# A four-layer graph network on one core: the first group's x loaded by rows and turned by TensorE, and layer 3's sums scaled on ScalarE instead of VectorE

## The chip, the core and the metric

The kernel runs on one core of a Trainium2 chip. The core has five engines that work side by side, each through its own queue in order: TensorE (PE, matrix products and transposes, written to PSUM), VectorE (DVE), ScalarE (ACT), GpSimd (POOL) and SyncE (SP, which here only issues DMAs). The profile gives the loading of TensorE's stationary operand a row of its own, PEld. The metric is the device time of one execution in microseconds (us). Before the change it is 2847.82 us, the median of 3 runs (2847.09 to 2848.99).

## What is computed

There are 128 graphs of 128 nodes with 256 features, and an adjacency matrix for each. Four layers follow one another; each ends in a residual sum and a layer norm.

```python
x = layernorm(x + gat(x, adj, L0_W, a_src, a_dst))       # attention of 4 heads, elu
x = layernorm(x + gated(x, adj, weight, w_ih, ...))      # 3 rounds: sum over neighbours, GRU cell
x = layernorm(x + relational(x, adj, weight, bias))      # adj == 1 .. 4, here only the value 1 occurs
# layer 3: attention of one head
Wh = einsum('bni,oi->bno', h, W)
e = leaky_relu((Wh @ a1)[:, :, None] + (Wh @ a2)[:, None, :], 0.2)
attention = softmax(where(adj > 0, e, -9e15), axis=-1)
x = layernorm(h + elu(einsum('bij,bjo->bio', attention, Wh)))
```

## The kernel before

The graphs are worked in 33 groups: one of 2 graphs, 31 of 4, one of 2. A group passes through stages that are Python generators: `loads` (its DMAs), `head` (layer 0), four interleaved lanes for layer 1 (`chunk_0`, `chunk_1` with the gates' elementwise work, `reset_and_new`, `new_and_update` with the gates' products, line 590), and `tail` (layers 2 and 3). Several groups are under way at once. Which stage of which group takes its next step is written out by hand as strings of letters: `START` for the beginning, `STEPS` for each of the periods in the middle, `END` for the end. `advance` takes one step, that is, runs a generator to its next `yield`. At the end every engine's instructions are tied to the order in which they were written (line 860), so no scheduler moves them: each engine does exactly what the strings say, in that order.

PSUM has eight banks. Two pairs hold the gates' sums (tags `sums` and `gate`); the other four (`OTHERS = 4`, line 26) form one ring under the tag `ps`, from which `bank()` hands out the next in turn, whoever asks. A tile of the ring may be written only when the reader of the tile four requests earlier is done. `psb` tiles (line 419) come out of the same ring.

Layer 0 needs x with features on the partitions. The method is the same for all groups: `load_x_squares` (line 151) issues eight DMAs that put 32x32 squares into `x0s`, so that a VectorE transpose within squares (line 437) gives xT; `head` multiplies xT by `w0` (line 450, TensorE), copies the result to `wh` (line 453, ScalarE), and goes on to scores, softmax and the weighted sum. `load_rows` (line 149) brings x by rows as well, for the residual. For the first group these loads are issued before all else on SP, while ScalarE's queue issues the loads of the weights (lines 182 to 222) before its first real work, which is `above` (line 443).

After the first products of the first group comes `fold` (line 269), which folds weights of layer 1 into one another; its first matmuls (line 276) multiply the loaded `w_hh` into the `sums` banks.

In layer 3, `tail` computes `em` (the unscaled exponentials) and `den` (their sums, then their reciprocals, line 801), turns `em` to `aT`, and multiplies it by `wh` for two graphs at a time into one `ps` bank (line 823). Line 826 scales this bank by the reciprocals into `o`, one VectorE operation of 128x512. `residual_elu_norm` then reads `o` (line 377, ScalarE).

Around line 826 other groups are at work. In the middle periods the two halves of a group are scaled at two places, some 6 us apart:

- The first stands on VectorE between line 353 (a norm's statistics) and line 618 (a gate's sum). On ScalarE that place lies between the `z` activation (line 642) and four exponentials of layer 0 (line 398), which are followed by `n` (line 654), `z` again and the norm's application to x2 (line 361, read by the products `rel` x `x2` of line 740).
- The second stands on VectorE between the scores of line 475 and line 394. On ScalarE that place lies between the copy of `h1N` (line 676, read by the neighbours' products of line 569, ps<-edge,h1N) and the two copies of `hr` (line 742, read by line 754).

Of the kernel before, what the change touches and what calls it, by code (L numbers as in the profile page):

```python
# [9 lines left out]
F32 = mybir.dt.float32  # L10
BF16 = mybir.dt.bfloat16
I32 = mybir.dt.int32
AF = mybir.ActivationFunctionType
ALU = mybir.AluOpType
AX = mybir.AxisListType

P = 128
N = 128
D = 256
C = D // P  # L20
# [60 lines left out]
def kernel(ctx: ExitStack, tc: tile.TileContext, a: dict, out: bass.AP):  # L81
    nc = tc.nc
# [8 lines left out]
    sp = ctx.enter_context(tc.tile_pool(name="work", bufs=1))  # L91
# [5 lines left out]
    def ring(pool, shape, dtype, tag, name, bufs):  # L97

        k = taken[tag] = (taken.get(tag, -1) + 1) % bufs
        return pool.tile(shape, dtype, tag=f"{tag}_{k}", name=name, bufs=1)  # L100

    def bank(*shape, tag="ps"):

        t = ring(pp, [P, 512], F32, tag, tag, OTHERS if tag == "ps" else GATES)
        n = 1
        for s in shape:
            n *= s
        if len(shape) == 1:
            return t[:, :n]
        names = "abcd"[: len(shape)]  # L110
        sizes = {k: s for k, s in zip(names[1:], shape[1:])}
        return t[:, :n].rearrange(f"p ({' '.join(names)}) -> p {' '.join(names)}", **sizes)

    def matmul(ps, lhsT, rhs, start=True, stop=True):
        nc.tensor.matmul(ps, lhsT, rhs, start=start, stop=stop)  # L115

    def transpose(ps, src):
        nc.tensor.transpose(ps, src, ident)  # L118
# [11 lines left out]
    def squares(t, src):  # L130


        for b in range(P // Q):
            nc.sync.dma_start(
                t[ts(b, Q)].rearrange("r (i s) -> r i s", s=Q),
                src.rearrange("(i r) m -> r i m", r=Q)[:, :, ts(b, Q)],
            )

    def load_adj(st):
        st["adj"] = ring(sp, [P, st["n"], N], I32, "adj", f"adj_{st['g']}", 3)  # L140
        nc.sync.dma_start(st["adj"], adj[st["graphs"]].rearrange("g n m -> n g m"))
# [5 lines left out]
    def load_rows(st):  # L147
        st["x0"] = sp.tile([P, st["n"], D], F32, tag="x0", name=f"x0_{st['g']}")
        nc.sync.dma_start(st["x0"], x[st["graphs"]].rearrange("g n d -> n g d"))

    def load_x_squares(st):
        st["x0s"] = sp.tile([P, C, st["n"] * N], F32, tag="x0s", name=f"x0s_{st['g']}")
        for c in range(C):
            squares(st["x0s"][:, c, :], x[st["graphs"]].rearrange("g n d -> (g n) d")[:, ts(c, P)])
# [12 lines left out]
    def layers():  # L167
        return {"layers": [{"h": {}, "a": {}, "gates": {}} for _ in range(L)], "h": {}}

    def state(g):  # L170
        by_pe = {"head": g == 0, "tail": g == NG - 1}
        return {"g": g, "graphs": spans[g], "n": sizes[g], "relations": 1, "by_pe": by_pe, **layers()}

    states = {0: state(0)}


    load_x_squares(states[0])
    load_adj(states[0])
    load_rows(states[0])

    w0 = cp.tile([P, C, D + 2 * H], F32, tag="w0", name="w0")
    nc.scalar.dma_start(w0[:, :, :D], a["L0_gnn_W"].rearrange("(c p) o -> p c o", p=P))
# [128 lines left out]
    def from_dram(t, d):  # L311

        squares(t, d)
        return t
# [117 lines left out]
    def head(st):  # L432

        g0, n, by_pe = st["g"], st["n"], st["by_pe"]["head"]
        xT = st["x0s"]
        flat = xT.rearrange("p c m -> p (c m)")
        nc.vector.transpose(flat, flat)  # L437
        yield
        nbias = absent(st["adj"], f"0_{g0}")
        yield  # L440
# [5 lines left out]
        for g in range(G):  # L446
            if g < n:
                ps = bank(D + 2 * H)
# [9 lines left out]
        den = ring(sp, [P, n * H], F32, "den0", f"den0_{g0}", 2)  # L458
        ems = {}
        for k in range(0, G, 2):  # L460
# [6 lines left out]
            for g in range(k, k + 2):  # L467
                ps = rows_of[g] = bank(H, N)
# [26 lines left out]
        y = ring(sp, [P, n, D], F32, "x1", f"x1_{g0}", 2)  # L495
        nc.vector.reciprocal(den, den)
        yield
        for k in range(0, G, 2):
# [5 lines left out]
            if by_pe:  # L504
                for j in range(2):
                    ps = bank(H, N)
# [3 lines left out]
            else:  # L510
                flat = aT.rearrange("p g h n -> p (g h n)")
# [3 lines left out]
            ps = bank(2, H, F)  # L515
# [170 lines left out]
    def tail(st):  # L686

        g0, n, x1, hT, relations = st["g"], st["n"], st["x1"], st["h"], st["relations"]
        by_pe = st["by_pe"]["tail"]
        if by_pe:  # L690
            yield
            yield
            y = sp.tile([P, n, D], F32, tag="x2", name=f"x2_{g0}")
            for c in range(C):
                ps = bank(n, N)
# [5 lines left out]
        else:  # L701
# [7 lines left out]
            y = sp.tile([P, n, D], F32, tag="x2", name=f"x2_{g0}")  # L709
            flat = from_dram(y.rearrange("p g d -> p (g d)"), d)  # L710
# [13 lines left out]
        flat = adj_T  # L724
        nc.vector.transpose(flat, flat)
        adj_T = adj_T.rearrange("p (g n) -> p g n", g=n)
        y = ring(sp, [P, n, D], F32, "x3", f"x3_{g0}", 2)
# [3 lines left out]
        for k in range(0, n, step):  # L731
# [5 lines left out]
            for c in range(C):  # L737
                ps = bank(step, relations, N)
# [8 lines left out]
            for pair in range(k, k + step, 2):  # L747
                graphs = range(pair, min(pair + 2, k + step))
                ps = bank(len(graphs), D)
# [26 lines left out]
        xT = st["x3T"]  # L776
        wh = sp.tile([P, n, D + 2], F32, tag="wh3", name=f"wh3_{g0}")
        for g in range(G):
            if g < n:
                ps = bank(D + 2)  # L780
# [9 lines left out]
        den = ring(sp, [P, n], F32, "den3", f"den3_{g0}", 2)  # L790
        ps = bank(n, N)
# [11 lines left out]
        if by_pe:  # L803
            yield
            yield
            ps = bank(n, N)
# [4 lines left out]
        else:  # L811
            d = to_dram(f"em3_{g0}", em)
            yield
            flat = from_dram(aT.rearrange("p g n -> p (g n)"), d)
# [3 lines left out]
        y = sp.tile([P, n, D], F32, tag="o", name=f"o_{g0}")  # L818
        for k in range(0, G, 2):
            if k < n:  # L820
                ps = bank(2, D)
                for g in range(k, k + 2):
                    matmul(ps[:, g - k, :], aT[:, g, :], wh[:, g, :D])
            yield
            if k < n:
                nc.vector.tensor_tensor(
                    y[:, k : k + 2, :], ps, den[:, k : k + 2].unsqueeze(2).to_broadcast([P, 2, D]), ALU.mult
                )
            yield
        yield from residual_elu_norm(y, "x3", st, "o", "3")  # L830
        nc.sync.dma_start(out[st["graphs"]].rearrange("g n d -> n g d"), st["o"])
# [1 line left out]


    STAGES = {"c": constants, "f": fold, "l": loads, "h": head, "t": tail}
    STAGES |= {"p": reset_and_new, "q": new_and_update, "u": chunk_0, "v": chunk_1}
    running = {}
# [36 lines left out]
    ps = bank(1)  # L874
# [4 lines left out]
    with tc.If(redo > 0):  # L879
        with tc.For_i(0, B, G) as first:  # L880

            graphs = bass.ds(first, G)

            st = {"g": "all", "graphs": graphs, "n": G, "relations": R, **layers()}
            st["by_pe"] = {"head": False, "tail": False}
            for stage in (loads, head):
                for _ in stage(st):
                    pass
            lanes = {which: STAGES[which](st) for which in "pquv"}
            for which, steps in [("u", 4), ("v", 6)] + IN_TURN * L:  # L890
                for _ in range(steps):
                    next(lanes[which], None)
            for _ in tail(st):
                pass
# [38 lines left out]
```

## Time and profile before

| | |
|---|---|
| median of 3 runs | 2847.82 us |
| the profiled execution | 2849.61 us |
| its span, first to last instruction | 2847.7 us |
| TensorE busy | 2744.5 us, 96% of the span |
| VectorE busy | 2290.5 us, 80% |
| ScalarE busy | 1734.5 us, 61% |
| GpSimd busy | 941.2 us, 33% |
| line 826 on VectorE | 64 times, 43.7 us, 683 ns each |
| line 437 for the first group | once, 0.71 us |

The profile follows one execution. The span is the time from its first to its last instruction. "Busy" adds up the time in which an engine worked; matmuls are pipelined, so that a matmul of 256 columns shows 0.38 us but the next one starts 0.22 us later. In a line of the timeline stand the start in us, the length, the engine, the line of the code, the operation, what it writes and reads (with buffer numbers left out), the shape and how many were merged; in brackets, how long the engine had been idle and which instruction released it. In a list of waits stand the waiting engine and line, the releasing one, the total of the waits in us, their number and the longest.

### The profile page before, as it was taken

Reading aid. Unit: us, or ns where it says so; the run is one execution under the profiler, and the core shown is the slowest. Engines: PE = TensorE matmul, PEld = TensorE weight load, DVE = VectorE, ACT = ScalarE, POOL = GpSimd, SP = SyncE. Lnnn points to the kernel's source line nnn. Section 1 sums busy time; section 2 is a strip of 40 time slices with the busy share of each in tenths; the row PEclk is TensorE's granted clock in tenths of the full one; section 3 lists DMA queues with packets and bytes.
Section 4 is the critical chain, followed back from the end, with each engine's and each line's share of the span. In section 5 each row is a group of like instructions: output and inputs, shape, how many; then the busy total and the mean of one; then the engine's idle time right before and its main releaser. Section 6 shows DMA issues by size and latency. Waiting matters only on the chain.

```text
span 2847.7 us, 44849 instructions
## 1 busy us (share of the span) xinstructions
PE 2744.5 (96%) x14486; PEld 2292.4 (81%) x14486; DVE 2290.5 (80%) x5334; ACT 1734.5 (61%) x4440; POOL 941.2 (33%) x925
## 2 busy tenths in 40 slices
PE   6899999999999999999999999999999999999986
PEld 4778888888888888888888888888888888888774
DVE  6678888878888878888878888888888887888765
ACT  3556666656666656666656666656666656666644
POOL 0223333323333323333323333423333333333331
PEclk9999999999999999999999999999999999999998
DMA  3344555444555344545344445444445444445321
GB/s 91 79 83 82 98 107 107 86 93 89 100 102 111 82 93 90 103 97 114 85 88 95 99 97 115 89 82 98 95 97 115 93 83 95 95 96 110 71 56 46
DMA packets 1179217, 264.01 MB, mean 93 GB/s; under 512 B 932065, under 2 KB 1178721, under 8 KB 1178977
## 3 DMA queue, kind: packets, MB, share of 16 engines
q1 hardware_dynamic: 1174448, 257.26, 45.1%
q10 hardware_dynamic: 4528, 3.81, 0.5%
q8 instruction: 118, 1.93, 0.3%
q14 instruction: 123, 1.00, 0.1%
HBM read 153.36 MB, written 107.61 MB: 92 GB/s over the span
## 4 chain that ended last, share of the span: by engine, by line
PE 75%; DVE 19%; issue 2%; POOL 1%; ACT 1%; DMA 1%; SPq 0%; DVEq 0%; POOLq 0%; ACTq 0%
PE gate L590 35%; PE ps L115 21%; PE sums L590 16%; DVE d L662 2%; PE ps L118 2%; DVE h3T L663 2%; DVE gate L618 2%; DVE h2T L663 2%; DVE n L652 1%; DVE aT L512 1%; DVE em L475 1%; DVE h0T L334 1%; DVE em L796 1%; POOL T_h L553 1%; DVE sums L610 1%
## 5 line engine op out<-in xcount | busy, mean ns | idle before, releaser
L590 PE MATMUL gate<-T_a,factors 128*128 128x256 f32 (+1 forms) x2376 | 683.1, 376 | 17.8 <-DVE T_a L553 16.9
L590 PE MATMUL gate<-T_h,factors_h 128*128 128x256 f32 (+1 forms) x2376 | 682.0, 377 | 12.3 <-DVE gate L618 8.9
L590 PEld LDWEIGHTS gate<-T_a,factors 128*128 128x128 f32 x2376 | 438.6, 190 | 91.1 <-DVE T_a L553 29.5
L590 PEld LDWEIGHTS gate<-T_h,factors_h 128*128 128x128 f32 x2376 | 428.8, 190 | 96.1 <-DVE gate L618 37.4
L590 PE MATMUL sums<-agT,factors 128*128 128x256 f32 (+1 forms) x1188 | 344.5, 376 | 2.3 <-ACT sums L600 1.4
L654 ACT ACTIVATE n<-n,bih 128x512 f32<-128x512 f32 (+1 forms) x198 | 139.5, 705 | 248.6 <-DVE n L652 248.6
L600 ACT COPY sums<-gate 128x256 f32<-128x256 f32 (+1 forms) x396 | 139.8, 353 | 204.7 <-PE gate L590 199.3
L361 ACT ACTIVATE x<-x,mr_x,rs_x 128x256 f32<-128x256 f32 x384 | 199.2, 589 | 90.9 <-DVE mr_x L356 90.9
L398 ACT ACTIVATE em<-em,nm 128x128 f32<-128x128 f32 x640 | 248.1, 392 | 8.3 <-DVE nm L395 5.4
L590 PEld LDWEIGHTS sums<-agT,factors 128*128 128x128 f32 x1188 | 219.5, 190 | 39.3 <-ACT agT L573 6.7
L657 POOL TENSOR_TENSOR d<-h1T,n 128x512 f32<-128x512 f32 (+1 forms) x66 | 82.1, 1245 | 499.9 <-ACT n L654 499.9
L715 POOL TENSOR_TENSOR x<-x,x 128x512 f32<-128x512 f32 x63 | 78.9, 1273 | 434.2 <-DVE x L712 411.0
L115 PE MATMUL ps<-wh,aT 128*128 128x64 f32 (+1 forms) x1280 | 191.0, 296 | 1.4 <-DVE aT L512 1.0
L657 POOL TENSOR_TENSOR d<-h2T,n 128x512 f32<-128x512 f32 (+1 forms) x66 | 92.7, 1405 | 276.9 <-ACT n L654 276.9
L590 PE MATMUL gate<-agT,factors 128*128 128x256 f32 (+1 forms) x594 | 180.5, 385 | 3.3 <-ACT r L642 2.5
L115 PEld LDWEIGHTS ps<-wh,aT 128*128 128x128 f32 x1280 | 170.7, 192 | 13.5 <-DVE aT L512 1.2
L650 DVE SCALAR_TENSOR_TENSOR n<-r,n 128x512 f32<-128x512 f32 (+1 forms) x198 | 132.2, 669 | 52.3 <-ACT n L648 52.2
L573 ACT COPY agT<-ps 128x512 f32<-128x512 f32 (+1 forms) x198 | 113.9, 575 | 97.5 <-PE ps L115 97.3
L354 POOL TENSOR_TENSOR rs_x<-rs_x,neghalf 128x4 f32<-128x4 f32 (+1 forms) x99 | 98.5, 995 | 217.1 <-DVE rs_x L353 217.0
L745 POOL TENSOR_TENSOR x<-x,b 128x256 f32<-128x256 f32 x128 | 138.4, 1110 | 68.3 <-PE ps L115 68.3
L610 DVE TENSOR_TENSOR sums<-gate,p_r 128x256 f32<-128x256 f32 (+1 forms) x99 | 42.0, 424 | 141.4 <-PE gate L590 141.3
L115 PE MATMUL ps<-w,x0s 128*128 128x264 f32 x512 | 139.2, 396 | 14.7 <-DVE x0s L437 14.7
(169 smaller groups left out, 6253.1 us busy)
## 6 DMA issues: line engine op xcount, KB each, us to landing
d_em<-em SPq DMA_DIRECT2D x63, 512.0 KB, 3.4
aT<-d_em SPq DMA_DIRECT2D x252, 128.0 KB, 3.9
x0s<-in_x_dram SPq DMA_DIRECT2D x248, 64.0 KB, 2.5
adj<-in_adj_dram SPq DMA_DIRECT2D x62, 256.0 KB, 3.9
x<-in_x_dram SPq DMA_DIRECT2D x31, 512.0 KB, 4.1
d_h0T<-x SPq DMA_DIRECT2D x62, 256.0 KB, 2.7
h0T<-d_h0T SPq DMA_DIRECT2D x124, 128.0 KB, 3.2
d_h<-h3T SPq DMA_DIRECT2D x62, 256.0 KB, 2.3
```

What stands on the lines that cost most here:

```text
L115: nc.tensor.matmul(ps, lhsT, rhs, start=start, stop=stop)
L354: nc.gpsimd.tensor_tensor(rs, rs, neghalf[:, :n], ALU.pow)
L361: nc.scalar.activation(y[:, g, :], y[:, g, :], AF.Identity, bias=mr[:, g : g + 1], scale=rs[:, g : g + 1])
L398: nc.scalar.activation(em[:, r, :], em[:, r, :], AF.Exp, bias=nm[:, i : i + 1], accum_out=den[:, i : i + 1])
L573: nc.scalar.copy(t, ps)
L590: nc.tensor.matmul(into, w[:, SEL[name], k - 1], layer[source][k], start=start, stop=True, skip_group_check=True)
L600: nc.scalar.copy(c11, c21)
L650: nc.vector.scalar_tensor_tensor(n, tr, 1.0, n, ALU.add, ALU.mult)
L654: nc.scalar.activation(n, n, AF.Tanh, bias=bih[:, 2 * C + c : 2 * C + c + 1])
L657: nc.gpsimd.tensor_sub(d, hT, n)
L663: nc.vector.scalar_tensor_tensor(hT, d, 0.5, n, ALU.mult, ALU.add)
L745: nc.gpsimd.tensor_add(x2[:, g, :], x2[:, g, :], b2)
```

## The change

Two things change. For the first group, x is loaded by rows only; `head` turns it with four TensorE transposes into two `ps` banks, and two ScalarE copies bring it to `x0s`. The eight DMAs of squares and the VectorE transpose of that group go away, and the load of the rows moves ahead of that of the adjacency. For every group, line 826's one VectorE operation on two graphs becomes two ScalarE activations (Copy, with the reciprocals as a per-partition scale), one for each graph, at the same place of the written order. The strings `START`, `STEPS` and `END` are not touched, and no other instruction changes its place on its engine.

```diff
--- before.py
+++ after.py
@@ -174,9 +174,8 @@
     states = {0: state(0)}
 
 
-    load_x_squares(states[0])
+    load_rows(states[0])
     load_adj(states[0])
-    load_rows(states[0])
 
     w0 = cp.tile([P, C, D + 2 * H], F32, tag="w0", name="w0")
     nc.scalar.dma_start(w0[:, :, :D], a["L0_gnn_W"].rearrange("(c p) o -> p c o", p=P))
@@ -432,9 +431,17 @@
     def head(st):
 
         g0, n, by_pe = st["g"], st["n"], st["by_pe"]["head"]
-        xT = st["x0s"]
-        flat = xT.rearrange("p c m -> p (c m)")
-        nc.vector.transpose(flat, flat)
+        if by_pe:
+            xT = sp.tile([P, C, n * N], F32, tag="x0s", name=f"x0s_{g0}")
+            for c in range(C):
+                ps = bank(n, N)
+                for g in range(n):
+                    transpose(ps[:, g, :], st["x0"][:, g, ts(c, P)])
+                nc.scalar.copy(xT[:, c, :].rearrange("p (g n) -> p g n", g=n), ps)
+        else:
+            xT = st["x0s"]
+            flat = xT.rearrange("p c m -> p (c m)")
+            nc.vector.transpose(flat, flat)
         yield
         nbias = absent(st["adj"], f"0_{g0}")
         yield
@@ -823,9 +830,8 @@
                     matmul(ps[:, g - k, :], aT[:, g, :], wh[:, g, :D])
             yield
             if k < n:
-                nc.vector.tensor_tensor(
-                    y[:, k : k + 2, :], ps, den[:, k : k + 2].unsqueeze(2).to_broadcast([P, 2, D]), ALU.mult
-                )
+                for g in range(k, k + 2):
+                    nc.scalar.activation(y[:, g, :], ps[:, g - k, :], AF.Copy, scale=den[:, g : g + 1])
             yield
         yield from residual_elu_norm(y, "x3", st, "o", "3")
         nc.sync.dma_start(out[st["graphs"]].rearrange("g n d -> n g d"), st["o"])
```

## Prediction

> **What bounds the kernel now.** I read the busy totals first, then the chain that ended last, then TensorE's waits in the steady part, then one period instruction by instruction.
>
> ```profile
> PE 2744.5 (96%) x14486; PEld 2292.4 (81%) x14486; DVE 2290.5 (80%) x5334; ACT 1734.5 (61%) x4440; POOL 941.2 (33%) x925
> PE 75%; DVE 19%; issue 2%; POOL 1%; ACT 1%; DMA 1%; SPq 0%; DVEq 0%; POOLq 0%; ACTq 0%
> ```
>
> TensorE is the bound; ScalarE, with room on average, is 1% of the chain. The work recurs every 85.1 us (L826 stands at 388.1, 473.2, 558.3 us). TensorE's and its weight loader's waits over 240 to 2700 us (total us, times, longest):
>
> ```profile
> PE gate L590 <- DVE T_a L553: 15.2, 29, 1.1
> PE gate L590 <- DVE gate L618: 5.1, 30, 0.4
> PE ps L118 <- DVE h2T L663: 4.6, 29, 0.2
> PEld ps L115 <- ACT h1N L676: 6.1, 29, 0.2
> ```
>
> Nothing there waits for L826. But once per period TensorE comes to ps<-edge,h1N just after ScalarE has copied h1N: 0.2 us of waiting, 29 times. So ScalarE sets TensorE's time at that one place. One period there, ScalarE's lines first, then the others:
>
> ```profile
> 1068.72 0.69 ACT L642 ACTIVATE z<-sums,bhalf 128x512 f32<-128x512 f32 x1 [1.90 <-PE sums L590]
> ...
> 1070.84 0.71 ACT L654 ACTIVATE n<-n,bih 128x512 f32<-128x512 f32 x1
> 1072.06 0.69 ACT L642 ACTIVATE z<-gate,bhalf 128x512 f32<-128x512 f32 x1 [0.51 <-PE gate L590]
> 1072.64 2.06 ACT L361 ACTIVATE x<-x,mr_x,rs_x 128x256 f32<-128x256 f32 x4
> 1074.61 0.36 ACT L600 COPY sums<-gate 128x256 f32<-128x256 f32 x1
> 1074.91 0.36 ACT L602 COPY p_nh<-gate 128x256 f32<-128x256 f32 x1
> 1075.17 0.57 ACT L676 COPY h1N<-ps 128x512 f32<-128x512 f32 x1
> 1075.64 1.12 ACT L742 COPY hr<-ps 128x512 f32<-128x512 f32 x2
> ...
> 1068.81 0.69 DVE L826 TENSOR_TENSOR o<-ps,den 128x512 f32<-128x512 f32 x1
> 1074.67 0.67 DVE L826 TENSOR_TENSOR o<-ps,den 128x512 f32<-128x512 f32 x1
> 1075.98 1.06 PE L115 MATMUL ps<-edge,h1N 128*128 128x128 f32 x8
> ```
>
> From 1072.06 to 1076.8 ScalarE has no gap. L826 runs at two sites: A (1068.81) and B (1074.67). A is over before TensorE needs its bank; B ends at 1075.34, 0.64 us before ps<-edge,h1N starts.
>
> **What the Trainium skill says.** *ScalarE: Activation LUTs*, "What ACT_TABLE_LOAD costs": an ACTIVATE takes 186 ns + 0.833 ns per element, about 93 ns more for each per-partition pointer operand, and neighbours overlap by about 93 ns. The trace agrees: L361 (256 elements, two pointers) should take 585 ns and took 589. *PSUM — Partial Sum Buffer*, "PSUM bank collisions raise a hardware error": guard by bank, so TensorE may not write a bank until its reader is done. *TensorE: Matmul & The Clock Gate*, "Step-by-step: what each phase is for": matmuls stay in program order, so a blocked one blocks all behind it; nothing in this trace contradicts it. *DMA: Bandwidth & Descriptors*, "Issuing engines are not separate DMA queues": SP's and ScalarE's loads share the same 16 engines; at 2 to 20 us their busy share here is 0.70 to 1.01.
>
> **The change, part by part.**
>
> *Price of the new operation.* Two activations of 128x256 out of PSUM, scale by pointer, for each L826 of 0.68 us. Nearest rows:
>
> ```profile
> L361 ACT ACTIVATE x<-x,mr_x,rs_x 128x256 f32<-128x256 f32 x384 | 199.2, 589 | 90.9 <-DVE mr_x L356 90.9
> L600 ACT COPY sums<-gate 128x256 f32<-128x256 f32 x372 | 133.7, 359 | 188.7 <-PE gate L590 183.6
> L648 ACT ACTIVATE n<-gate,bhn 128x256 f32<-128x256 f32 x6 | 2.8, 468 | 0.0
> ```
>
> L648 has one pointer and reads PSUM: 0.47 us, and I take it. Floor: a copy, 0.36. Ceiling: two pointers, 0.56. With the overlap a pair takes 0.76 us of the queue (0.54; 0.94).
>
> *Site A.* In the built order the pair stands behind z<-sums and ahead of four em exponentials. Those move from 1069.30 to 1070.06, n from 1070.84 to 1071.60. z<-gate, 0.62 later, starts at 1072.22 instead of 1072.06: the 0.51 us gap and the overlap absorb all but 0.16 (floor 0, ceiling 0.34). L361 and h1N behind it are 0.16 late; L361 feeds ps<-rel,x, which has no slack. VectorE's L826 here gives nothing back: L618 behind it at 1069.58 waits for a matmul ending at 1069.54.
>
> *Site B, the main term.* The pair stands right behind h1N. Counting the ps tiles in TensorE's order from site B's product: h1T transposes +1, two ps<-rel,x +2 and +3, ps<-edge,h1N +4. The ring has four banks (OTHERS), so ps<-edge,h1N writes the bank that the pair reads. Before, its first matmul waits for VectorE and ScalarE; in the changed program for ScalarE alone. The pair ends at 1075.17 + 0.47 (h1N's pitch) + 0.38 + 0.47 = 1076.49; h1N's end to first matmul is 0.24 now, so TensorE starts at 1076.73 instead of 1075.98: 0.75 late (floor 0.53, ceiling 0.93). Queued behind the pair are the hr copies, at 1076.36 instead of 1075.64; ps<-w,hr needs them only after 0.9 us of edge matmuls, so that lateness lies inside the stall.
>
> *Given back.* VectorE loses 1.37 us per period, but each VectorE stall above follows a VectorE operation that itself waited for TensorE after site B (T_a at 1051.89: an unbroken run from L652 at 1042.15, which had waited 1.29 for a matmul). Those runs move with TensorE. I take 0.
>
> *Steady sum.* 0.75 + 0.16 = 0.91 per group, groups 1 to 28: 25.5 us (floor 14.8, ceiling 35.6).
>
> *Groups 29 to 32.* In group 29 site A has no gap (z<-gate follows n directly), so 0.76 passes through: 0.7 + 0.75 = 1.45. Group 30: the pair precedes L600 and an h1N copy, 0.5. Around 2821 six activations now precede L361 where two multiplies on VectorE did: x2 about 0.5 later for the last group, though VectorE's statistics come earlier. Last: 0.85 for 0.73. About 2.6 together (1 to 4).
>
> *Start.* Gone are eight 32 KB loads in 128-byte pieces and a VectorE transpose (0.71). Added: four TensorE transposes, done by about 5 us while TensorE is idle, and two ScalarE copies (0.37 each), which queue behind all of ScalarE's weight-load issues and the table load:
>
> ```profile
> 14.66 3.88 PE L115 MATMUL ps<-w,x0s 128*128 128x264 f32 x8 [14.66 <-DVE x0s L437]
> 19.05 1.28 ACT L443 ACT_TABLE_LOAD   x1 [19.05 <-DMA w<-in_L_gnn_W_dram]
> ```
>
> Each load waits for an older one on the same of eight completion semaphores, SP's and ScalarE's mixed. With 33 loads ScalarE issued its last at 18.54. By count (25 now) it would be at 12.8; by data (those pieces held the engines 1.7 us) at about 16.7. I take 15.0, the queue free at 15.5: table to 16.8, first copy to 17.2, matmuls 17.3 to 21.2 instead of 14.66 to 18.55. The sums matmuls began at 19.60 behind the w_hh loads and took 3.75 at half speed (those at 24.2 run twice as fast). Now they follow without a gap and may speed up midway: end near 23.6 against 23.35, so +0.2; from -2 (queue free early) to +3.5 (queue no earlier). On SP, x, adj and adj_s move ahead; the next group's eight loads wait for matmuls ending at 21.2 instead of 18.55 and would land near 29, wanted at 42.06. That cover is 13 us.
>
> Total: 25.5 + 2.6 + 0.2 = 28.3. The profiled execution took 2849.61 for a span of 2847.7 (1.9 around it), 1.8 above the median of 2847.82; I add to the median: 2876.
>
> **Rivals.**
> Cheap pair: the activation costs what a copy does; 14.8 + 1.6 + 0.2 gives 2864. For it: PSUM reads are the quicker ones; against: L648.
> Dear pair: two pointers or a wait between the two; 35.6 + 4 + 0 to 2 gives 2888.
> Other bank: if my count of the ring is off, site B stalls nobody; 0.16 x 28 + 2.6 + 0.2 gives 2855. Against: the waits of the built programs.
> Faster: VectorE's relief reaches the T_a stall (0.52 per period of TensorE idle, at 1051.89, 15.2 in all) while site B does not hold. Then 2855 - 15 = 2840. It decides only if VectorE's run into T_a starts earlier; above 0.91 returned per period it would win even with site B's stall. For it: VectorE is 19% of the chain. Against: that run starts at a TensorE wait.
> The change may also miss its aim at the start, if ScalarE's queue is no earlier; that is the +3.5, inside the range.
>
> **How the numbers follow.** Forecast 0.66, cheap 0.12, dear 0.11, other bank 0.05, faster 0.04, a cancelling to no change 0.02. Within 0.2% (5.7 us) is what a measurement here can't tell from no change. Slower 0.94, same 0.02, faster 0.04. The range runs from between other bank and cheap to just past dear: 2858 to 2889, leaving out about one in ten.
>
> **What would show it.** Right: ScalarE's o pair at 0.45 to 0.49 each; ps<-edge,h1N starting 0.2 to 0.3 after the second of them; a new TensorE wait for ScalarE's o, some 29 times about 0.7; TensorE busy the same with the span up; VectorE's idle time up. Wrong: ps<-edge,h1N still right behind h1N, T_a's wait shrinking, or a period not about 0.9 longer.

## The result, and the profile after

The changed kernel takes 2870.70 us (median of 4 runs, 2870.21 to 2871.09); the kernel before, in the same runs, 2848.40 us (2847.09 to 2850.07). The ratio is 1.0078 with a 95% interval of 1.006 to 1.0095: 22.3 us slower. The profiled execution took 2870.97 us for a span of 2869.2.

The page of the changed kernel, busy totals and then the chain that ended last:

```profile
PE 2752.7 (96%) x14490; PEld 2290.2 (80%) x14490; DVE 2263.9 (79%) x5269; ACT 1774.3 (62%) x4570; POOL 931.2 (32%) x925
PE 72%; DVE 19%; ACT 4%; issue 2%; POOL 1%; DMA 1%; SPq 0%; ACTq 0%; DVEq 0%; POOLq 0%
```

VectorE is busy 26.6 us less and ScalarE 39.8 us more. TensorE is the bound as before, but ScalarE's share of the chain went from 1% to 4%. Where it enters stands in the waits of the changed kernel from 240 to 2720 us (total us, times, longest):

```profile
PEld ps L115 <- ACT o L834: 16.9, 29, 0.6
PE gate L597 <- DVE T_a L560: 15.1, 29, 1.1
PE ps L115 <- ACT o L834: 11.4, 29, 0.4
PEld ps L115 <- ACT x L360: 5.8, 29, 0.2
```

The waits for `o` are new (line 834 is the new activation): once per period TensorE and its weight loader stand for it. The last line is site A's: before, the weight loader waited for this x (line 361 there) once, 0.2 us in all, and now it does so in every period. T_a, 15.2 us before, is 15.1: the work taken off VectorE shortened no wait of TensorE for VectorE by more than 0.3 us in all.

ScalarE's timeline of one period of the changed kernel; it shows site A in the first three lines and site B in the last three:

```profile
1074.33 0.69 ACT L649 ACTIVATE z<-sums,bhalf 128x512 f32<-128x512 f32 x1 [1.89 <-PE sums L597]
1074.91 0.83 ACT L834 ACTIVATE o<-ps,den 128x256 f32<-128x256 f32 x2
1075.62 0.41 ACT L397 ACTIVATE em<-em,nm 128x128 f32<-128x128 f32 x1
...
1077.17 0.71 ACT L661 ACTIVATE n<-n,bih 128x512 f32<-128x512 f32 x1
1077.78 0.67 ACT L649 ACTIVATE z<-gate,bhalf 128x512 f32<-128x512 f32 x1
1078.35 2.07 ACT L360 ACTIVATE x<-x,mr_x,rs_x 128x256 f32<-128x256 f32 x4
...
1080.89 0.58 ACT L683 COPY h1N<-ps 128x512 f32<-128x512 f32 x1
1081.36 0.83 ACT L834 ACTIVATE o<-ps,den 128x256 f32<-128x256 f32 x2
1082.08 1.07 ACT L749 COPY hr<-ps 128x512 f32<-128x512 f32 x2
```

The gap of 0.51 us ahead of the second `z` is used up. At site B the pair stands between h1N and hr and ends at 1081.36 + 0.83 = 1082.19. TensorE at the same place, the changed kernel first, the kernel before below:

```profile
1079.63 2.23 PE L115 MATMUL ps<-rel,x 128*128 128x128 f32 x16
1082.24 1.16 PE L115 MATMUL ps<-edge,h1N 128*128 128x128 f32 x8 [0.39 <-ACT o L834]
1083.24 1.89 PE L115 MATMUL ps<-w,hr 128*128 128x256 f32 x8
```

```profile
1074.02 2.12 PE L115 MATMUL ps<-rel,x 128*128 128x128 f32 x16
1075.98 1.06 PE L115 MATMUL ps<-edge,h1N 128*128 128x128 f32 x8
1076.87 1.89 PE L115 MATMUL ps<-w,hr 128*128 128x256 f32 x8
```

ps<-edge,h1N starts 0.05 us after the pair has ended. From the start of ps<-rel,x to that of ps<-w,hr it took 2.85 us and now takes 3.61: 0.76 more. (The 0.39 in brackets is less than the delay, since it counts from the modelled end of the product before, and in a stream matmuls overlap.)

Where the 21.5 us between the two spans lie, from the starts of the same VectorE instructions in both traces:

| stretch | added, us |
|---|---|
| start, up to 30 us | 0.0 |
| 30 to 118 us, TensorE at half clock for a shorter time | -1.3 |
| groups 1 to 28, 0.76 each | +21.3 |
| group 29 | +1.3 |
| around 2720 us, half clock before, none after | -1.3 |
| the rest, to the end | +1.5 |

### The profile page after: what moved, and what is told of

It reads as the page before. It is cut to its first block, busy times and chain, and to the rows that moved or that the text cites. A ratio compares the mean times of both kernels' runs of the same rounds, so it can differ in the third digit from the quotient of the medians.

```text
span 2869.2 us, 44818 instructions
## 1 busy us (share of the span) xinstructions
PE 2752.7 (96%) x14490; PEld 2290.2 (80%) x14490; DVE 2263.9 (79%) x5269; ACT 1774.3 (62%) x4570; POOL 931.2 (32%) x925
## 4 chain that ended last, share of the span: by engine, by line
PE 72%; DVE 19%; ACT 4%; issue 2%; POOL 1%; DMA 1%; SPq 0%; ACTq 0%; DVEq 0%; POOLq 0%
PE gate L597 34%; PE ps L115 19%; PE sums L597 16%; DVE d L669 2%; PE ps L118 2%; DVE gate L625 2%; DVE h3T L670 2%; DVE h2T L670 2%; DVE n L659 1%; DVE aT L519 1%; DVE em L482 1%; DVE h0T L333 1%; DVE em L803 1%; POOL T_h L560 1%; ACT o L834 1%
## 5 line engine op out<-in xcount | busy, mean ns | idle before, releaser
L597 PE MATMUL gate<-T_a,factors 128*128 128x256 f32 (+1 forms) x2376 | 682.5, 376 | 17.9 <-DVE T_a L560 17.0
L752 POOL TENSOR_TENSOR x<-x,b 128x256 f32<-128x256 f32 x128 | 127.3, 1022 | 68.3 <-PE ps L115 68.3
```

What stands on the lines that cost most here:

```text
L597: nc.tensor.matmul(into, w[:, SEL[name], k - 1], layer[source][k], start=start, stop=True, skip_group_check=True)
L752: nc.gpsimd.tensor_add(x2[:, g, :], x2[:, g, :], b2)
```

## The experiments

A *slope* below is what a kernel adds per period to the kernel before, from the starts of the same VectorE instructions in both traces between 465 and 2660 us. It leaves out the start, the end and the spells of half clock, which vary from execution to execution. The kernel before ran 33 times beside e1 to e4 (median 2847.15 us) and 33 times beside e5, e6, e8 and e9 (2846.89).

**The two halves of the change.** e1 takes the first two parts of the diff (the loads and `head`), e2 the last one alone.

```diff
-    load_x_squares(states[0])
-    load_adj(states[0])
     load_rows(states[0])
+    load_adj(states[0])
...
+        if by_pe:
+            xT = sp.tile([P, C, n * N], F32, tag="x0s", name=f"x0s_{g0}")
...
```

```diff
-                nc.vector.tensor_tensor(
...
+                for g in range(k, k + 2):
+                    nc.scalar.activation(y[:, g, :], ps[:, g - k, :], AF.Copy, scale=den[:, g : g + 1])
```

> Only the start is changed: the first group's x by rows, turned by TensorE; layer 3 is scaled on VectorE as before. My theory: the start costs nothing from 24 us on (TensorE's transposes of w1 0.05 us later), and the 1.3 to 1.7 us that the changed kernel gained between 54 and 61 us come from where TensorE's half-speed spell happened to fall, not from the change. So 2848.4 +- 1.5, with no new wait in the steady part and a period of 85.1 us. Rival: the head brings the whole change, or the 1.3 us are its own; then at least 1 us below the kernel before in the same runs.

> Only layer 3's scaling moves to ScalarE; the start is as before. My theory: all of the loss is here, 0.77 us in each of 28 periods and some 3 us in the last groups: 2871 to 2873, with a TensorE wait for ScalarE's o 29 times. Rival (the new head delays something later): 2860 or less.

Measured: e1 2847.31 us (2845.44 to 2850.40), ratio 1.0004 (0.9995 to 1.0012), slope 0.00. e2 2873.04 us (2870.31 to 2874.59), ratio 1.009 (1.0075 to 1.0106), slope 0.81. The new head changes nothing that these runs can tell (-1.4 to +3.4 us), and the scaling on ScalarE is the whole loss. The 1.3 us that the table above credits to the stretch up to 118 us need not be the head's: e1's median shows no such gain, and kernels with the old head differ as much there (last section). That e2's slope is 0.05 above the changed kernel's comes from single periods, since the median period adds 0.77 in both.

**The two sites apart.** e3 moves the first half of each group (k = 0, site A) to ScalarE and leaves the other on VectorE; its edit is shown. e4 has `k == 2` in its place (site B).

```diff
-                nc.vector.tensor_tensor(
...
+                if k == 0:
+                    for g in range(k, k + 2):
+                        nc.scalar.activation(y[:, g, :], ps[:, g - k, :], AF.Copy, scale=den[:, g : g + 1])
+                else:
+                    nc.vector.tensor_tensor(
...
```

> Only the first two graphs of each group (site A) are scaled on ScalarE, the second two on VectorE. My theory (the bank at site B decides): ScalarE's queue is about 0.12 us late at the h1N copy and nothing else; 28 x 0.12 = 3.4 at most, with about 1 us in the last groups: 2849 to 2853, no wait for o. Rival (the load on ScalarE decides, wherever it falls): half of the loss, 2860. Rival (VectorE's relief is worth something): below 2848.

> Only the second two graphs of each group (site B) are scaled on ScalarE. My theory: 0.77 less the 0.12 of site A, 0.65 in each of 28 periods = 18.2, and 1 to 2 us in the last groups: 2866 to 2869, TensorE waits for o 29 times. Rival (load): 2860.

Measured: e3 2849.85 us (2847.06 to 2852.73), ratio 1.001 (1.0003 to 1.0016), slope 0.12. e4 2867.58 us (2865.05 to 2868.74), ratio 1.0072 (1.0056 to 1.0087), slope 0.67. Together 0.79, against 0.76 and 0.81 with both. TensorE's timeline, e3 first, then e4:

```profile
1074.12 2.23 PE L115 MATMUL ps<-rel,x 128*128 128x128 f32 x16
1076.19 1.06 PE L115 MATMUL ps<-edge,h1N 128*128 128x128 f32 x8
1077.08 1.89 PE L115 MATMUL ps<-w,hr 128*128 128x256 f32 x8
```

```profile
1079.85 2.12 PE L115 MATMUL ps<-rel,x 128*128 128x128 f32 x16
1082.37 1.16 PE L115 MATMUL ps<-edge,h1N 128*128 128x128 f32 x8 [0.40 <-ACT o L828]
1083.37 1.89 PE L115 MATMUL ps<-w,hr 128*128 128x256 f32 x8
```

In e3 the products ps<-rel,x take 2.23 instead of 2.12 us, since the activation that feeds them (line 361) runs late: the weight loader waits for it 29 times, 5.7 us in all. Nothing waits for `o`. In e4 they take 2.12, and ps<-edge,h1N comes 2.52 us after their start instead of 1.96. The two delays are separate things, and the second is the larger.

**Is it the bank, or ScalarE's queue?** In e4 either is possible: the pair holds the bank that ps<-edge,h1N is to write, and it also sits in ScalarE's queue. e5 is e4 with the banks of two requests exchanged: ps<-edge,h1N takes the next bank of the ring, and the request after it (ps<-w,hr) the one that was passed over. Instructions and order stay.

```diff
+        if tag in passed:
+            k = passed.pop(tag)
+        else:
+            k = taken[tag] = (taken.get(tag, -1) + 1) % bufs
+            if swap.pop(tag, None):
+                passed[tag] = k
+                k = taken[tag] = (k + 1) % bufs
...
         n = src.shape[1]
+        if c == 0 and name.startswith("1_"):
+            swap["ps"] = True
         ps = bank(n, N)
```

> As the kernel with only the second half on ScalarE, but the neighbours' product ps<-edge,h1N takes the bank of the h1T transposes, and the following ps<-w,hr takes the bank that the scaling reads: the two change places in the ring. The same instructions in the same order. My theory (the bank wait is the cause): TensorE runs ps<-edge,h1N at once; what is late next is the second hr copy behind the pair, about 0.2 us per period: 28 x 0.2 + 1.5 = 7, so 2853 to 2858, with the wait for o gone and a smaller one for hr in its place. Rival (the pair delays ScalarE's queue, the bank is beside the point): no change against the second half alone, 2866 to 2869.

Measured: 2856.49 us (2854.23 to 2859.96), ratio 1.0035 (1.0022 to 1.0049), slope 0.31 instead of e4's 0.67. ScalarE's and then TensorE's timeline of e5:

```profile
1075.30 0.58 ACT L685 COPY h1N<-ps 128x512 f32<-128x512 f32 x1
1075.77 0.84 ACT L837 ACTIVATE o<-ps,den 128x256 f32<-128x256 f32 x2
1076.50 1.08 ACT L751 COPY hr<-ps 128x512 f32<-128x512 f32 x2
```

```profile
1076.10 1.06 PE L122 MATMUL ps<-edge,h1N 128*128 128x128 f32 x8
1077.14 2.05 PE L122 MATMUL ps<-w,hr 128*128 128x256 f32 x8
```

The product now starts at 1076.10, in the middle of the pair (1075.77 to 1076.61): with another bank it need not wait for it. What is late next is hr, behind the pair in ScalarE's queue. In e5's waits over 240 to 2720 us, `o` is gone and this stands there:

```profile
PEld ps L122 <- ACT hr L751: 10.5, 57, 0.2
```

Some 0.18 us twice per period, where one wait of about 0.2 was expected: ps<-w,hr starts 0.15 later behind ps<-edge,h1N than before and takes 2.05 instead of 1.89 us, which together is the slope of 0.31. So the bank is the cause of e4's stall, and what is left is the queue's share, which the stall had covered.

**The dose.** e6 is e4 with the second activation of the pair done twice. The extra one computes nothing new.

```diff
                         nc.scalar.activation(y[:, g, :], ps[:, g - k, :], AF.Copy, scale=den[:, g : g + 1])
+                    nc.scalar.activation(y[:, k + 1, :], ps[:, 1, :], AF.Copy, scale=den[:, k + 1 : k + 2])
```

> As the kernel with only the second half on ScalarE, with a third activation behind the two (the last graph scaled once more, with the same result). My theory: ps<-edge,h1N waits for the last of them, one pitch of 0.36 us more in each of 28 periods: 10 us above the second half alone, 2876 to 2879. Rival (the stall is a fixed cost of a wait, not the length of the pair): within 3 us of the second half alone.

Measured: 2882.14 us (2879.66 to 2883.06), ratio 1.0122 (1.0106 to 1.0137), slope 1.19, which is 0.52 above e4's. e6's timeline, ScalarE and then TensorE:

```profile
1083.34 0.85 ACT L828 ACTIVATE o<-ps,den 128x256 f32<-128x256 f32 x2
1084.22 0.47 ACT L829 ACTIVATE o<-ps,den 128x256 f32<-128x256 f32 x1
```

```profile
1084.75 1.16 PE L115 MATMUL ps<-edge,h1N 128*128 128x128 f32 x8 [0.91 <-ACT o L829]
```

TensorE again starts 0.06 us after the last reader of the bank (1084.69), so it follows that reader to the end, wherever that is. The size was missed: in the pair the second activation starts 0.36 us after the first, but the third only 0.03 us after the end of the second, whose tile it writes again. It cost its full 0.47 us and a gap, not the 0.36 us from start to start in a pair. That the tile written twice is the reason is likely, but no run separates it.

**The same pair, elsewhere on ScalarE.** e9 is e4 with one letter of `STEPS` moved: the step that scales the second half comes 17 letters earlier, so that the pair stands between `n` and `z`, in ScalarE's 0.51 us gap, and not behind h1N.

```diff
-eggbdbibdfcdiiicfgggibeiicbdilbbiifciiickiidgddfiddfgddegfffffieggemginifdfcfibcgifcbdldlcclifffdgge
+eggbdebibdfcdiiicfgggibiicbdilbbiifciiickiidgddfiddfgddegfffffieggemginifdfcfibcgifcbdldlcclifffdgge
```

> As the kernel with only the second half on ScalarE, but in the middle periods its pair is written 17 steps earlier, behind n's tanh, into the 0.5 us in which ScalarE waits for TensorE. Same operations on the same engines. My theory: the bank is free 5 us before ps<-edge,h1N wants it; ScalarE is 0.1 us late at z<-gate, as at site A. 28 x (0 to 0.12) + 1.5: 2849 to 2853. Rival (load on ScalarE, wherever it falls): as the second half alone, 2866 to 2869.

Measured: 2852.08 us (2848.57 to 2853.75), ratio 1.0019 (1.0012 to 1.0026), slope 0.11. The profiled run was the fastest of its 19. ScalarE's timeline of e9, and TensorE's below it:

```profile
1067.66 0.71 ACT L654 ACTIVATE n<-n,bih 128x512 f32<-128x512 f32 x1
1068.28 0.82 ACT L828 ACTIVATE o<-ps,den 128x256 f32<-128x256 f32 x2
1068.99 0.68 ACT L642 ACTIVATE z<-gate,bhalf 128x512 f32<-128x512 f32 x1
1069.56 2.07 ACT L361 ACTIVATE x<-x,mr_x,rs_x 128x256 f32<-128x256 f32 x4
```

```profile
1070.84 2.23 PE L115 MATMUL ps<-rel,x 128*128 128x128 f32 x16
1072.90 1.06 PE L115 MATMUL ps<-edge,h1N 128*128 128x128 f32 x8
1073.80 1.89 PE L115 MATMUL ps<-w,hr 128*128 128x256 f32 x8
```

ps<-edge,h1N is back at 2.06 us after ps<-rel,x, and no wait for `o` is left. The same two activations on the same engine cost 5.2 us where e4's cost 20.4 (each against the median of the kernel before beside it). What remains is what e3 showed: ps<-rel,x takes 2.23, fed late by line 361.

**The head without ScalarE's queue.** e8 is e1 with the two copies of `head` on VectorE; layer 3 is as before.

```diff
-                nc.scalar.copy(xT[:, c, :].rearrange("p (g n) -> p g n", g=n), ps)
+                nc.vector.tensor_copy(xT[:, c, :].rearrange("p (g n) -> p g n", g=n), ps)
```

> The new head with its two PSUM copies on VectorE instead of ScalarE, layer 3 on VectorE as before. VectorE is free from 10.2 us, so the first products start near 11 us instead of 17.9, and the sums matmuls only wait for w_hh, at about 17.8 instead of 21.6 (19.6 before the change). My theory: the start is 1.8 to 3 us shorter than before and the gain stays to the end: 2845 to 2847. Rival: the weights' loads or the fold set the start anyway: 2848.4 +- 1.

Measured: 2845.46 us (2842.76 to 2850.37), ratio 0.9993 (0.9985 to 1.0002): the median is 1.4 us lower, within what the interval allows for no change, so the gain of 1.8 to 3 us that was expected is not shown. TensorE at the start of e8:

```profile
11.83 3.89 PE L115 MATMUL ps<-w,x0s 128*128 128x264 f32 x8 [6.34 <-DVE x0s L440]
18.69 3.78 PE L115 MATMUL sums<-factors_h,ident 128*128 128x512 f32 x4 [2.96 <-DVE factors_h L265]
```

The first products start at 11.83 instead of 14.66, but the next ones wait until 18.69 for the preparation of `w_hh` (19.60 before). Of 2.8 us gained, 0.9 reach them. By 30 us 0.2 are left, because TensorE ran at half speed for longer in this execution (ps<-wih,w1T took 6.09 us, 5.43 before); that varies without the change, as the next section shows, so the trace doesn't tell what of the 0.9 would stay. What these sums wait for is the weights, not the first group's products. No experiment gave a version that is clearly faster than the kernel before.

## Why the prediction was right, and where its sizes were off

*The price of the activation* (0.47 us, 0.76 of the queue): the group of the changed kernel reads

```profile
L834 ACT ACTIVATE o<-ps,den 128x256 f32<-128x256 f32 x128 | 53.5, 475 | 6.5 <-PE ps L115 6.5
```

475 ns each, and the second of a pair starts 0.36 us after the first (0.83 - 0.475), so that a pair takes 0.71 to 0.72 us of the queue. The row with the same form (one pointer, out of PSUM) was the right one to take; the cheap and the dear pair fall. The Trainium skill, *ScalarE: Activation LUTs*, "What ACT_TABLE_LOAD costs", gives 186 + 0.833 x 256 + 93 = 492 ns and an overlap of 93; measured are 17 less, and 0.12 us of overlap. The measurement decides.

*Site B, the main term* (0.75 per period): the mechanism was right, and e4, e5, e6 and e9 show it from four sides. It holds 0.65. h1N's pitch came as taken (0.47), the pair ended 0.02 sooner, and the rest lies in the 0.24 from the reader's end to TensorE's first matmul. That number was read off h1N, which the product *loads as weights*: before, the weight load starts 0.13 after h1N's end (1075.74) and the matmul 0.11 after that. The weight loader's timeline there, the kernel before:

```profile
1075.87 0.97 PEld L115 LDWEIGHTS ps<-edge,h1N 128*128 128x128 f32 x8
```

For a bank to come free, the record of the first matmul starts 0.05 after the reader's end, is 0.10 longer than its neighbours, and the product behind it comes 0.11 later than in a stream: in effect 0.16. A wait for an operand was taken as the price of a wait for a bank. (The weight load's record starts together with the matmul's, so that the trace doesn't tell whether the weights had been there before.)

*Site A* (0.16): 0.11 in the changed kernel's timeline, 0.12 as e3's slope. The pair took 0.71 us of the queue (1074.91 to 1075.62) instead of 0.76; the gap and the overlap absorbed 0.60, as taken.

*Given back* (0): T_a's wait stays at 15.1, and at 15.0 to 15.2 in e2 to e6 and e9. With it falls the rival in which VectorE's relief wins; the other-bank rival falls with e5.

*hr lies inside the stall*: right, as the changed kernel has no wait for it; e5, in which the stall is gone, shows the 0.18 us waits that it covered. (The prediction's 1076.36 for hr should be 1076.40 by its own 0.76; nothing hangs on it.)

*Steady sum* (0.91 x 28 = 25.5): 0.76 x 28 = 21.3. This is the mis-sized term: 4.2 of the 5.3 us between the forecast of 2876 and the 2870.7 measured. It consists of 0.08 (reader to matmul), 0.05 (the pair's share of the queue at site A) and 0.02 (its end at site B) per period.

*Groups 29 to 32* (2.6): +1.3 for group 29 (1.45 forecast) and +1.5 after it (1.1), together 2.8.

*Start* (+0.2): 0.0, but by luck, as two errors cancel. The changed kernel's ScalarE and TensorE there:

```profile
15.69 0.48 ACTq L221 DMA_DIRECT2D b<-in_L_gnn_bias_dram  x1
16.19 1.28 ACT L440 ACT_TABLE_LOAD   x1 [16.19 <-DMA w<-in_L_gnn_W_dram]
17.49 0.65 ACT L440 COPY x0s<-ps 128x256 f32<-128x256 f32 x2
```

```profile
17.91 3.89 PE L115 MATMUL ps<-w,x0s 128*128 128x264 f32 x8 [12.33 <-ACT x0s L440]
21.59 1.99 PE L115 MATMUL sums<-factors_h,ident 128*128 128x512 f32 x4
```

ScalarE's queue was free at 16.2, not 15.5, so the products came at 17.9 instead of 17.3. The sums behind them ran at full speed throughout (1.99 us) and ended at 23.6, the time forecast. That speed is not shown to come from the change. With the new head the same sums took 2.82 us in e1; with the old head they took 3.75 in the kernel before, but 1.95 in e3 and e6. The kernel before, then e3:

```profile
19.60 3.75 PE L115 MATMUL sums<-factors_h,ident 128*128 128x512 f32 x4 [1.05 <-issue]
```

```profile
19.41 1.95 PE L115 MATMUL sums<-factors_h,ident 128*128 128x512 f32 x4 [0.78 <-issue]
```

The covers named for the other loads held: by 30 us nothing is late.

*The signs*: of those named, the pair's price and the new wait, 29 times, came true. ps<-edge,h1N starts 0.05 after the pair and not 0.2 to 0.3, and the waits are 0.4 and 0.6 long, not 0.7. TensorE's busy time was to stay and rose by 8.2 us, in part because the records beside the wait got longer (1.16 instead of 1.06, 2.23 instead of 2.12).

*Not in the prediction*: the two spells of half clock, -1.3 us each between these two profiled executions. They belong to executions, as the last section shows; they make the profiled difference (21.5) look smaller than the periods and the ends alone (24.1).

## What to carry to other kernels

Before moving a reader of PSUM to another engine, look at what stands ahead of it in that engine's queue, and count the ring: which product takes this bank next, and when does it start? A reader that is second in the queue behind the operand of that very product delays it by most of its own length (0.65 of 0.83 us here) in every period, on an engine that is 61% busy; the same instructions 17 letters earlier cost a quarter of that (5.2 us instead of 20.4). And read the price of a wait from a wait of its own kind: for a bank, not for an operand.

## What the runs showed of the hardware that had not been expected

In all ten traces TensorE stands idle for 2.9 us at the same place of the program (in the kernel before no matmul runs from 50.0 to 52.9 us). In eight of them the granted clock then drops to half for a spell, whose length differs between executions of the same instructions. Windows of 2 us (length, busy time and count of PE, PEld, DVE, ACT, POOL; then clock, DMA share, GB/s), the kernel before first, then the changed one, then e5:

```profile
54.00:56.00 2.00, 2.00 (x16) 1.78 (x15) 1.92 (x4) 1.10 (x4) 1.76 (x3) 0.58 0.78 143
56.00:58.00 2.00, 2.00 (x12) 1.80 (x11) 1.94 (x8) 0.00 (x0) 0.48 (x2) 0.50 0.27 81
```

```profile
54.00:56.00 2.00, 2.00 (x12) 2.00 (x10) 1.75 (x4) 1.04 (x3) 1.55 (x3) 0.51 0.82 150
56.00:58.00 2.00, 1.90 (x19) 1.48 (x17) 1.54 (x7) 0.66 (x3) 0.63 (x2) 1.00 0.25 71
```

```profile
54.00:56.00 2.00, 2.00 (x22) 1.76 (x20) 1.86 (x4) 1.04 (x4) 1.83 (x4) 1.00 0.87 176
```

Over the traces the spell lasted 0 us (e5, e9), 3.4 (the changed kernel, e1, e6), 6.8 (before, e2, e4) or 10.2 (e3, e8). That is in steps of 3.4, which agrees with the Trainium skill, *TensorE: Matmul & The Clock Gate*, "What's actually happening": the clock follows a free-running window of 3413 ns. The steps also tell the traces with a spell from those without. Laid out from the clock's rise at the start (23.6 us in the kernel before, 24.05 in e5), one step holds 1.85 us (e2) to 2.93 us (e1) of the idle time in each of the eight, and the spell begins where that step ends (54.32 in the kernel before). In e5 and e9 a border between two steps cuts the idle time, and neither holds more than 1.62 us. This is inferred from ten traces; why a spell then lasts one, two or three steps stays open.

Some 2.7 us of a profiled time hang on the spell (e5 is 0.1 us ahead of the kernel before at 45 us and 2.7 at 60 us). The start varies as well: e3 and e9, whose head is the old one, are 2.2 us ahead of the kernel before at 30 us. At 60 us e9 is 4.9 us ahead of it, with nothing changed in that part, so single executions can't be compared closer than some 5 us; a slope over periods can.
